# A two-layer graph attention kernel: v's last products moved up, both ends of the step loop written out anew

## The chip, the cores and the metric

The kernel runs on one core of a Trainium2 chip. The metric is device time of one execution in microseconds (us), as the median of several runs. Times inside the kernel are in us from the start of the profiled execution's span.

## The reference, cut to what matters

The input is x, 128 graphs of 128 nodes with 512 features, in float32, and an adjacency mask adj (128 x 128 for each graph). Two layers follow one another; each adds masked attention to its input and normalises the sum.

```python
# layer 0: 4 heads of 64          layer 1: 8 heads of 64, mask = adj | eye, h = layernorm(x)*gamma + beta
q, k, v = split_heads(x @ Wq), split_heads(x @ Wk), split_heads(x @ Wv)
sim  = einsum('bhid,bhjd->bhij', q, k) * 64**-0.5
attn = softmax(where(mask, sim, very_negative), axis=-1)
out  = einsum('bhij,bhjd->bhid', attn, v).reshape(...) @ Wo + bo
x    = layernorm(x + out)
```

Layer 1 computes q, k and v from a second layernorm of its input (h) with one matrix w_qkv, and its output goes through w_out. All of it is float32.

## The kernel before, in words

**Tiling.** The 128 graphs form 64 groups of two. A group's rows R[g] lie in SBUF as 128 nodes by 2 by 512. Every large product (q, k, v and the output projections) is computed by a scheme of seven products instead of eight (Strassen-Winograd): GpSimd forms sums of the left halves (`xs` and `so`, in `halves_sums`), VectorE forms differences of the weights once (`weight_sums`, `weight_sums_out`), TensorE runs products 1 to 7, and ScalarE and VectorE combine the results while they take them out of PSUM. The table `INTO` says which PSUM bank a product goes to: 1, 6, 7 and 4 accumulate one after another in bank "a", 5 and 3 in bank "f", 2 in a bank of a shared ring of four. After 1 and 6 (and 5) ScalarE copies the bank out; after 7 VectorE adds the bank to an earlier copy; after 4 ScalarE copies the bank again (`taken`, L349). So 6, 7 and 4 each wait until the engine that reads bank a after the one before has read it, and the next product 1 in that bank waits for the copy after 4. Layer 1 has `product` for q and k ("qk": banks qka, qkc, qkf in the trace) and v ("va", "vc", "vf"), layer 0 has `product_0` (all three at once: a, c, f), and the projections have `out_product` (oa, oc, of), whose seven results VectorE adds to R[g] one by one (L418).

**Stages.** The loop runs over s, 2 to 67, and each `step(s)` works on several groups at once: layer 0's q, k and v of group s, its attention (scores, masks, exponentials) of group s-1, its output and norm of group s-2, layer 1's qk of group s-2 and v of group s-3, layer 1's attention of group s-3 and its output and norm of group s-4. A step has two halves, for graph k = 2s and k = 2s+1 of the attentions.

**The attention of one graph.** `scores` fills two PSUM banks per layer. `masked` has GpSimd fill a tile sm with the very negative number (memset, L458), VectorE copy the scores over it where the mask is set (L460), and VectorE take the maximum (L463). `exps` is ScalarE's exponentials with their sums. `normalised` is a reciprocal on VectorE (L484) and a multiplication on GpSimd (L485). `blocks` turns the probabilities in 32 x 32 blocks on VectorE and writes them to DRAM (`put`), `probs_arrive` reads them back with partitions and blocks exchanged (`fetch`, tile pT), which completes the transposition. `attend` (av) multiplies pT by v; ScalarE copies the result to aT.

**The transposition of rows** goes the same way: `turn` (VectorE, L212) and a write, `arrive` the read back (tile raw), and ScalarE puts it in order: `in_order` for layer 0 (L239), `finish` for layer 1, where it also applies gamma and beta (L252), in two halves; both end with GpSimd's sums. At the ends, where the round trip has no other work beside it, `finish_direct` transposes on TensorE instead (ht).

**Order.** The schedule is written out by hand: each engine executes its instructions in the order in which the program calls them, and semaphores are set for the dependences between engines. Most work buffers (sm, xT1, raw, the sums) exist once, so a writer waits for the last reader of the group before. `finish` of the next group overwrites xT1, which v's product 4 of the group before still reads. `flush()` carries out deferred norms on ScalarE, `flush(latest)` deferred ratios on GpSimd. All DMAs are issued by SyncE, in program order.

Of the kernel before, what the change touches and what calls it, by code (L numbers as in the profile page):

```python
# [10 lines left out]
F32 = mybir.dt.float32  # L11
# [6 lines left out]
P = 128  # L18
# [9 lines left out]
def kernel(ctx: ExitStack, tc: tile.TileContext, x, adj, wq, wk, wv, wo, bo,  # L28
# [27 lines left out]
    def flush(what=later):  # L56
        while what:
            what.pop(0)()
# [95 lines left out]
    wsqk = const.tile([P, 3, KH, 2, I1 // 2], F32, name="wsqk")  # L154
    wsv = const.tile([P, 3, KH, I1 // 2], F32, name="wsv")

    def weight_sums(w, ws):
        for c in range(KH):
            if w is w1qk:
                b11, b12 = w[:, c, :, 0], w[:, c, :, 1]  # L160
                b21, b22 = w[:, KH + c, :, 0], w[:, KH + c, :, 1]
            else:
                b11, b12 = w[:, c, 0], w[:, c, 1]
                b21, b22 = w[:, KH + c, 0], w[:, KH + c, 1]
            combine(b11, b12, b21, b22, ws[:, 0, c], ws[:, 1, c], ws[:, 2, c])

    def combine(b11, b12, b21, b22, t2, t3, t4):
        nc.vector.tensor_sub(b12, b12, b11)
        nc.vector.tensor_sub(t2, b22, b12)
        nc.vector.tensor_sub(t3, t2, b11)  # L170
        nc.vector.tensor_sub(t4, b21, t2)

    def weight_sums_0():
        combine(*(w0[:, c:c + KH, h].rearrange("p c t f -> p c (t f)") for c in (0, KH) for h in range(2)),
# [253 lines left out]
    def scores(k):  # L428
        both = members(k)
        made = []  # L430
        for l, g, b in both:
            H_ = HEADS[l]

            ps = [mm_tile(f"sc{l}_{g}_{b}_{s}").rearrange("p (k n) -> p k n", n=N) for s in range(2)]
            t = slice(b * N, (b + 1) * N)
            for h in range(H_):
                r = slice((h % 2) * D, (h % 2 + 1) * D)
                if l == 0:
                    q_, k_ = (QKV[g][r, b, h // 2, i, :] for i in range(2))
                else:  # L440
                    q_, k_ = (QK[1, g][r, i * H_ // 2 + h // 2, t] for i in range(2))
                nc.tensor.matmul(ps[h % 2][:, h // 2, :], q_, k_, start=True, stop=True)  # L442
            made.append((l, g, b, ps))
        return made

    def with_self(g):

        if 0 <= g < NG:
            nc.vector.tensor_tensor(M[g], M[g], eye[:, None, :].to_broadcast([P, G, N]), op=ALU.max)

    def masked(made, layer):
        for l, g, b, ps in made:
            if l != layer:
                continue
            K = HEADS[l] // 2
            mask = M[g][:, b, :]
            sm = two.tile([P, 2, K, N], F32, tag=f"sm{l}", bufs=1, name=f"sm{l}_{g}_{b}")
            nc.gpsimd.memset(sm, (NEG0, NEG1)[l])  # L458
            for s in range(2):
                nc.vector.copy_predicated(sm[:, s], mask[:, None, :].to_broadcast([P, K, N]),  # L460
                                          ps[s][:, :K, :])
            nmax = three.tile([P, 2, K], F32, tag=f"nmax{l}", name=f"nmax{l}_{g}_{b}")
            nc.vector.tensor_reduce(nmax, sm, AX.X, ALU.max, negate=True)  # L463
            total = three.tile([P, 2, K], F32, tag=f"total{l}", name=f"total{l}_{g}_{b}")
            SM[l, g, b], SUM[l, g, b], NMAX[l, g, b] = sm, total, nmax

    def exps(l, k):
        b = k % G
# [10 lines left out]
    def normalised(k):  # L479
        for l, g, b in members(k):  # L480
            K = HEADS[l] // 2
            sm = SM[l, g, b]
            rec = three.tile([P, 2, K], F32, tag=f"rec{l}", name=f"rec{l}_{g}_{b}")
            nc.vector.reciprocal(rec, SUM.pop((l, g, b)))  # L484
            nc.gpsimd.tensor_tensor(sm, sm, rec[:, :, :, None].to_broadcast([P, 2, K, N]),  # L485
                                    op=ALU.mult)
# [38 lines left out]
    def probs_arrive(k):  # L525
        if members(k):
            fetch(*SCR.pop(("p", k)))
# [25 lines left out]
    def out_sums(l, g):  # L553
        if not 0 <= g < NG:
            return
        K = HEADS[l] // 2
        so = SO[l, g] = one.tile([P, 4, K // 2, N], F32, tag=("so", "xs0")[l], name=f"so{l}_{g}")
        halves_sums(so, AT[l, g].rearrange("p b (h c) n -> p b h c n", h=2))
# [63 lines left out]
    def p(kind, g, *which):  # L622
        for i in which:
            product(kind, g, i)

    def opening():

        transposed(0)

        for h in range(2):  # L630
            nc.scalar.activation(w0[:, :, h, 0, :], w0[:, :, h, 0, :], AF.Copy, scale=SCALE)
        product_0(0, 1)
        weight_sums_0()
        product_0(0, 2, 5, 6, 3)
        made = scores(2)
        masked(made, 0)
        exps(0, 2)
        product_0(0, 7, 4)
        normalised(2)
        blocks(2, 0, 1)  # L640
        made = scores(3)
        masked(made, 0)
        exps(0, 3)
        for _ in range(4):
            setup.pop(0)()
        load(2)
        transposed(1)
        product_0(1, 1, 5)
        normalised(3)
        blocks(3, 0, 1)  # L650
        probs_arrive(2)
        probs_arrive(3)
        for _ in range(4):
            setup.pop(0)()
        product_0(1, 2, 6, 3)
        while setup:
            setup.pop(0)()
        weight_sums_out(0)
        product_0(1, 7, 4)
        transposed(2)  # L660

    def step(s):
        k = 2 * s

        direct = s in (2, NG, NG + 1)
        load(s + 1)
        made = scores(k)
        masked(made, 0)
        masked(made, 1)
        exps(0, k)  # L670
        addend(0, s - 2)
        with_self(s - 2)
        p("qk", s - 3, 4)
        product_0(s, 1)
        attend(s)
        exps(1, k)
        out_sums(0, s - 2)
        if s >= NG:
            out_sums(1, s - 4)
        product_0(s, 5, 2)  # L680
        out_product(0, s - 2, 1, 5, 2)
        if s < NG:
            normalised(k)
            addend(1, s - 4)
            out_product(0, s - 2, 6)
            product_0(s, 6)
            blocks(k, 0)
            out_product(0, s - 2, 3, 7)
            stats(0, s - 2, 0)
            product_0(s, 3)  # L690
            out_product(0, s - 2, 4)
            stats(0, s - 2, 1)
            product_0(s, 7)
            p("v", s - 3, 1)
            blocks(k, 1)
            p("v", s - 3, 2)
            flush()
            p("v", s - 3, 5)
        else:
            p("v", s - 3, 1)  # L700
            out_product(0, s - 2, 6, 3)
            p("v", s - 3, 2)
            out_product(0, s - 2, 7)
            stats(0, s - 2, 0)
            p("v", s - 3, 5)
            out_product(0, s - 2, 4)
            stats(0, s - 2, 1)
            normalised(k)
            if s < NG + 3:
                addend(1, s - 4)  # L710
            flush()
            blocks(k, 0, 1)
        if not direct:
            turn(1, s - 2)
            arrive(1, s - 2)
        k += 1
        made = scores(k)
        masked(made, 0)
        if s == 2:
            weight_sums(w1qk, wsqk)  # L720
        p("v", s - 3, 6)
        product_0(s, 4)
        if s >= NG:
            p("v", s - 3, 3, 7, 4)
        if direct:
            finish_direct(s - 2)
        exps(0, k)
        masked(made, 1)
        exps(1, k)
        if s < NG:  # L730
            p("v", s - 3, 3)
            out_sums(1, s - 4)
        if s == NG + 2:
            addend(1, NG - 1)
        flush(latest)
        out_product(1, s - 4, 1, 5, 2)
        if s < NG:
            p("v", s - 3, 7)
        out_product(1, s - 4, 6, 3)
        if not direct:  # L740
            finish(s - 2, 0)
        if s < NG:
            p("v", s - 3, 4)
        normalised(k)
        turn(0, s + 1)
        probs_arrive(k - 1)
        if not direct:
            finish(s - 2, 1)
        out_product(1, s - 4, 7)
        stats(1, s - 4, 0)  # L750
        if s < NG + 2:
            blocks(k, 0, 1)
        else:
            blocks_direct(k)
        arrive(0, s + 1)
        if s < NG + 2:
            probs_arrive(k)
        p("qk", s - 2, 1)
        out_product(1, s - 4, 4)
        stats(1, s - 4, 1)  # L760
        p("qk", s - 2, 2, 5, 6)
        in_order(s + 1)
        if s != NG + 2:
            flush()
        p("qk", s - 2, 3, 7)
        if s == 2:
            weight_sums(w1v, wsv)
            weight_sums_out(1)

    opening()  # L770
    for s in range(2, NG + 4):
        step(s)


# [27 lines left out]
```

## Time and profile before

| What | Value |
|---|---|
| Time, median of 3 runs | 2950.45 us (2949.8 to 2950.89) |
| Span of the profiled execution | 2946.6 us, 63045 instructions, TensorE clock 0.99 |
| VectorE, ScalarE, GpSimd busy | 62%, 51%, 59% |
| DMA engines | 139 GB/s mean, 408.36 MB |
| One step in mid-run | 44.36 us (scores at 1424.52 and again at 1468.88) |
| Steps 2 and 3 (from scores to scores) | 48.43 to 86.18, 86.18 to 136.29 us |
| Steps 64 to 67 | from 2799.73 us to the end |

How to read it: a step in the middle is all work of 64 steps, so a microsecond there counts some 60 times and one at the ends once. The timeline rows shown below give the start and the duration of a merged group of instructions, the engine, the line, output tile and inputs, the count, and in brackets how long the engine was idle before them and what ended that. In rows of TensorE's waits the numbers are the total in us, how many times, and the longest. Rows of windows give busy time and instructions of TensorE, weight loads, VectorE, ScalarE and GpSimd, then the granted TensorE clock, the DMA share and GB/s.

### The profile page before, as it was taken

What the parts mean: (1) busy time and instruction counts of PE and PEld (TensorE: products, weight loads), DVE (VectorE), ACT (ScalarE), POOL (GpSimd) and SP (SyncE); (2) the same over time, 40 slices, a digit from 0 to 9 for tenths busy, and PEclk for the clock granted to TensorE, in tenths of its full rate; (3) what the DMA queues carried; (4) which work ended last, traced back from release to release, by engine and by line L of the source; (5) the groups of instructions that cost most, each with busy time, mean ns of one, the idle gap of its engine ahead of it and who ended that gap; (6) DMA issues with size and microseconds to landing.
All of it is one profiled execution on the core that took longest, in us unless ns stands there. A gap on an engine that the chain in (4) does not pass through costs nothing.

```text
span 2946.6 us, 63045 instructions
## 1 busy us (share of the span) xinstructions
PE 2846.1 (97%) x23289; PEld 2623.1 (89%) x23289; DVE 1832.0 (62%) x3623; ACT 1496.9 (51%) x4811; POOL 1752.4 (59%) x2439
## 2 busy tenths in 40 slices
PE   7899999999999999999999999999999999999986
PEld 7799999999989989999989989999999999999975
DVE  4566666666666666665666665666666666665643
ACT  3355555555555455454554555555555555455443
POOL 2466566566566566566666566566566566566643
PEclk9899999999999999999999999999999999999988
DMA  4344544544544544544545545545545545545421
GB/s 142 112 142 136 155 133 143 158 130 141 160 129 142 158 131 138 164 128 140 166 124 144 162 124 148 160 126 148 159 127 148 157 129 148 156 129 148 136 65 58
DMA packets 243427, 408.36 MB, mean 139 GB/s; under 512 B 40104, under 2 KB 176304, under 8 KB 243120
## 3 DMA queue, kind: packets, MB, share of 16 engines
q1 hardware_dynamic: 243120, 404.33, 46.1%
q8 instruction: 185, 3.03, 0.4%
q14 instruction: 122, 1.00, 0.1%
HBM read 206.57 MB, written 197.66 MB: 137 GB/s over the span
## 4 chain that ended last, share of the span: by engine, by line
PE 89%; ACT 3%; DVE 2%; POOL 2%; DMA 1%; issue 1%; SPq 1%; ACTq 0%; POOLq 0%; DVEq 0%
PE qka L321 15%; PE a L377 11%; PE oa L414 10%; PE va L321 8%; PE qkf L321 7%; PE f L377 6%; PE sc L442 6%; PE av L546 6%; PE of L414 6%; PE vf L321 4%; PE qkc L321 4%; PE c L377 3%; PE oc L414 3%; ACT xT L252 2%; PE vc L321 2%; DMA raw<-scr 1%
## 5 line engine op out<-in xcount | busy, mean ns | idle before, releaser
L476 ACT ACTIVATE sm<-sm,nmax 128x128 f32<-128x128 f32 x1536 | 595.1, 396 | 268.4 <-DVE nmax L463 268.4
L485 POOL TENSOR_TENSOR sm<-sm,rec 128x512 f32<-128x512 f32 (+1 forms) x256 | 370.7, 1468 | 486.8 <-DVE rec L484 486.8
L284 POOL TENSOR_TENSOR xs<-xT 128x256 f32<-128x256 f32 x256 | 187.0, 730 | 431.2 <-ACT xT L239 382.4
L460 DVE COPY_PREDICATED sm<-m,sc 128x512 f32<-128x512 uint8 (+1 forms) x512 | 269.6, 579 | 204.5 <-POOL sm L458 200.1
L567 POOL TENSOR_TENSOR r<-r,bias 128x1024 f32<-128x1024 f32 x128 | 303.3, 2369 | 7.2 <-ACT r L566 7.2
L476 ACT ACTIVATION_READ_ACCUMULATOR sm<-sm,nmax 128x1 f32 x1536 | 298.3, 194 | 0.0
L503 DVE STREAM_TRANSPOSE turned<-sm 128x512 f32<-128x512 f32 (+1 forms) x255 | 243.5, 970 | 50.7 <-POOL sm L485 50.1
L418 DVE TENSOR_TENSOR r<-oa,r 128x256 f32<-128x256 f32 x512 | 213.7, 417 | 71.8 <-PE oa L414 69.3
L321 PE MATMUL qkf<-xs,w 128*128 128x128 f32 x2048 | 251.3, 276 | 3.2 <-POOL xs L284 3.2
L321 PE MATMUL qka<-xs,wsqk 128*128 128x128 f32 x2048 | 249.7, 275 | 0.0
L463 DVE TENSOR_REDUCE nmax<-sm 128x4 f32<-128x512 f32 (+1 forms) x256 | 243.9, 953 | 8.8
L321 PEld LDWEIGHTS qkf<-xs,w 128*128 128x128 f32 x2048 | 240.5, 193 | 3.4 <-POOL xs L284 3.4
L321 PEld LDWEIGHTS qka<-xs,wsqk 128*128 128x128 f32 x2048 | 239.1, 192 | 0.0
L347 ACT COPY ev<-va 128x256 f32<-128x256 f32 x128 | 47.5, 371 | 354.8 <-PE va L321 354.8
L352 DVE TENSOR_TENSOR qk<-qkf,eqk 128x512 f32<-128x512 f32 x64 | 44.3, 691 | 295.0 <-PE qkf L321 295.0
L414 PE MATMUL oa<-wso,so 128*128 128x256 f32 x768 | 215.1, 389 | 11.7 <-DVE r L418 11.7
L284 POOL TENSOR_TENSOR so<-aT 128x128 f32<-128x128 f32 (+1 forms) x256 | 151.4, 592 | 116.8 <-ACT aT L551 106.1
L612 ACT ACTIVATE r<-r,shift,root 128x512 f32<-128x512 f32 x256 | 194.3, 806 | 50.4 <-POOL shift L601 50.4
L414 PE MATMUL of<-wo,so 128*128 128x256 f32 x768 | 210.3, 383 | 0.8 <-POOL so L284 0.8
L252 ACT ACTIVATE xT<-raw,gb 128x256 f32<-128x256 f32 x244 | 133.2, 594 | 108.9 <-PE va L321 108.6
L458 POOL MEMSET sm<- 128x512 f32 (+1 forms) x256 | 181.5, 738 | 0.8 <-DVE turned L503 0.8
L414 PEld LDWEIGHTS oa<-wso,so 128*128 128x128 f32 x768 | 142.5, 192 | 43.6 <-issue 26.2
(140 smaller groups left out, 6583.5 us busy)
## 6 DMA issues: line engine op xcount, KB each, us to landing
scrp<-turned SPq DMA_DIRECT2D x124, 768.0 KB, 4.3
pT<-scrp SPq DMA_DIRECT2D x496, 192.0 KB, 4.4
scr<-turned SPq DMA_DIRECT2D x122, 512.0 KB, 3.0
raw<-scr SPq DMA_DIRECT2D x488, 128.0 KB, 3.2
r<-in_x_dram SPq DMA_DIRECT2D x64, 512.0 KB, 3.7
out_dram<-r SPq DMA_DIRECT2D x64, 512.0 KB, 2.9
m<-in_adj_dram SPq DMA_DIRECT2D x64, 32.0 KB, 3.5
raw_r<-in_L_gnn_w_qkv_dram SPq DMA_DIRECT2D x8, 256.0 KB, 4.0
```

The source lines that it names most:

```text
L284: nc.gpsimd.tensor_tensor(o, a0, a1, op=op)
L321: nc.tensor.matmul(o, lhsT, rhs, start=first and n == 0, stop=n == len(todo) - 1, skip_group_check=True)
L377: nc.tensor.matmul(acc[:, t * P:(t + 1) * P], lhsT, rhs, start=first and n == 0, stop=n == len(todo) - 1, skip_group_check=True)
L414: nc.tensor.matmul(acc, left[:, c], right[:, c], start=first and c == 0, stop=c == hk - 1, skip_group_check=True)
L418: nc.vector.tensor_add(part, acc, part)
L460: nc.vector.copy_predicated(sm[:, s], mask[:, None, :].to_broadcast([P, K, N]), ps[s][:, :K, :])
L463: nc.vector.tensor_reduce(nmax, sm, AX.X, ALU.max, negate=True)
L476: nc.scalar.activation(sm[:, s, k, :], sm[:, s, k, :], AF.Exp, bias=nmax[:, s, k:k + 1], accum_out=total[:, s, k:k + 1])
L485: nc.gpsimd.tensor_tensor(sm, sm, rec[:, :, :, None].to_broadcast([P, 2, K, N]), op=ALU.mult)
L503: nc.vector.transpose(t[:, :, lo:hi, :], sm)
L567: nc.gpsimd.tensor_tensor(R[g], R[g], (bias0, bias1)[l][:, None, :].to_broadcast([P, G, E]), op=ALU.add)
L612: nc.scalar.activation(R[g][:, b], R[g][:, b], AF.Identity, bias=shift[:, b:b + 1], scale=root[:, b:b + 1])
```

## The change

It rewrites the order of the step and touches no arithmetic. In steps 4 to 63: layer 1's v products 7 and 4 move ahead of the output products 5 and 2; the copy of v's last quarter so comes ahead of all of `finish` on ScalarE; the second half's reciprocals come after two of the output adds instead of five; the turn of the next group's rows follows three more adds; the first graph's probabilities are loaded at the end of the first half instead of in the second; the memsets of both layers are issued with the scores (`cleared`); the deferred ratios come after `finish`; qk's product 2 comes ahead of output product 4, and the first statistics follow the turned blocks.

At the start: in step 2 the exponentials follow `attend`, and w's differences are split in two parts; steps 2 and 3 both use `finish_direct` (before: step 2 only), with the turn and load of the next rows ahead of it. At the end, `closing(s)` takes the place of the branches for s >= 64: reciprocals ahead of the last products of v and of the statistics, norms behind ScalarE's copy of v's product 6, memsets of both layers ahead of the addend, and in step 66 masks and exponentials ahead of the addends, the last statistics of that step deferred to step 67.

The purpose is that bank a and the masks be free before the work that needs them.

```diff
-    def weight_sums(w, ws):
-        for c in range(KH):
...
+    def weight_sums(w, ws, *parts):
+        for part in parts:
+            for c in range(KH):
...
+    def combine_1(b11, b12, b21, b22, t2, t3, t4):
         nc.vector.tensor_sub(b12, b12, b11)
         nc.vector.tensor_sub(t2, b22, b12)
+
+    def combine_2(b11, b12, b21, b22, t2, t3, t4):
         nc.vector.tensor_sub(t3, t2, b11)
         nc.vector.tensor_sub(t4, b21, t2)
...
+    def cleared(made, *layers):
+
+        for l, g, b, ps in made:
+            if l in layers:
+                sm = SM[l, g, b] = two.tile([P, 2, HEADS[l] // 2, N], F32, tag=f"sm{l}", bufs=1,
+                                            name=f"sm{l}_{g}_{b}")
+                nc.gpsimd.memset(sm, (NEG0, NEG1)[l])
...
     def masked(made, layer):
...
-            sm = two.tile([P, 2, K, N], F32, tag=f"sm{l}", bufs=1, name=f"sm{l}_{g}_{b}")
-            nc.gpsimd.memset(sm, (NEG0, NEG1)[l])
+            sm = SM[l, g, b]
...
     def step(s):
         k = 2 * s
 
-        direct = s in (2, NG, NG + 1)
+        direct = s in (2, 3)
         load(s + 1)
         made = scores(k)
+        cleared(made, 0, 1)
...
         attend(s)
+        if s == 2:
+            exps(0, k)
+        exps(1, k)
...
+        if not direct:
+            turn(1, s - 2)
+            arrive(1, s - 2)
+            probs_arrive(k)
+        k += 1
+        made = scores(k)
+        cleared(made, 0, 1)
+        masked(made, 0)
+        p("v", s - 3, 6)
+        product_0(s, 4)
+        if direct:
+            turn(0, s + 1)
+            arrive(0, s + 1)
+            probs_arrive(k - 1)
+            p("v", s - 3, 3, 7, 4)
+            finish_direct(s - 2)
+        exps(0, k)
+        masked(made, 1)
+        if s == 2:
+            weight_sums(w1qk, wsqk, combine_1)
+        exps(1, k)
+        if not direct:
+            p("v", s - 3, 3)
+        out_sums(1, s - 4)
+        out_product(1, s - 4, 1)
+        if not direct:
+            p("v", s - 3, 7)
+        out_product(1, s - 4, 5)
+        if not direct:
+            p("v", s - 3, 4)
+            finish(s - 2, 0)
+        normalised(k)
+        out_product(1, s - 4, 2, 6, 3)
+        if not direct:
+            finish(s - 2, 1)
+            turn(0, s + 1)
+        flush(latest)
+        if s == 2:
+            weight_sums(w1qk, wsqk, combine_2)
+        out_product(1, s - 4, 7)
+        blocks(k, 0, 1)
+        if not direct:
+            arrive(0, s + 1)
+        probs_arrive(k)
+        stats(1, s - 4, 0)
+        p("qk", s - 2, 1, 2)
+        out_product(1, s - 4, 4)
+        stats(1, s - 4, 1)
+        p("qk", s - 2, 5, 6)
...
+    def closing(s):
...
+        if s == NG + 3:
+            stats(1, s - 5, 1)
         out_product(0, s - 2, 1, 5, 2)
...
+        p("v", s - 3, 1)
+        out_product(0, s - 2, 6, 3)
+        normalised(k)
...
         made = scores(k)
+        p("v", s - 3, 6)
+        flush()
+        cleared(made, 0, 1)
         masked(made, 0)
...
+        if s == NG + 2:
+            masked(made, 1)
+            exps(1, k)
+        if s < NG + 3:
+            addend(1, s - 4)
         if s == NG + 2:
             addend(1, NG - 1)
+        p("v", s - 3, 3, 7, 4)
+        if s < NG + 2:
+            finish_direct(s - 2)
+            exps(0, k)
+            masked(made, 1)
+            exps(1, k)
         flush(latest)
...
+        if s != NG + 2:
+            stats(1, s - 4, 1)
...
     opening()
-    for s in range(2, NG + 4):
+    for s in range(2, NG):
         step(s)
+    for s in range(NG, NG + 4):
+        closing(s)
```

## The prediction

> **What bounds the kernel now.** I read the busy table first: TensorE 2846.1 of 2946.6 us, and 89% of the chain of waits. Then TensorE's waits, then one step's timeline, then both ends. The rows:
>
> ```profile
> PE 2846.1 (97%) x23289; PEld 2623.1 (89%) x23289; DVE 1832.0 (62%) x3623; ACT 1496.9 (51%) x4811; POOL 1752.4 (59%) x2439
> ...
> PE qka L321 <- ACT v L349: 38.0, 61, 3.5
> PE oa L414 <- DVE r L418: 12.3, 5, 6.0
> PE va L321 <- DVE v L352: 7.9, 4, 4.9
> ```
>
> One wait, 38.0 us in 61 times (one of 3.5), is the largest. In TensorE's and ScalarE's timelines of a middle step:
>
> ```profile
> 1410.28 1.03 PE L321 MATMUL va<-wsv,xT 128*128 128x256 f32 x4
> 1411.14 1.03 PE L414 MATMUL oa<-wso,so 128*128 128x256 f32 x4
> 1412.74 2.05 PE L321 MATMUL qka<-xT,w 128*128 128x128 f32 x16 [0.57 <-ACT v L349]
> ...
> 1411.34 1.09 ACT L252 ACTIVATE xT<-raw,gb 128x256 f32<-128x256 f32 x2 [1.81 <-PE va L321]
> 1412.34 0.35 ACT L349 COPY v<-va 128x256 f32<-128x256 f32 x1
> 1412.59 1.09 ACT L252 ACTIVATE xT<-raw,gb 128x256 f32<-128x256 f32 x2
> ```
>
> The last product of v (4) fills bank a; the copy that frees it stands on ScalarE behind two activations of the next group's xT, which themselves waited for that product (they overwrite the xT it reads). qka, next in bank a, starts 0.05 us after the copy. From 1000 to 1500 us TensorE is busy 493.3 of 500: 1.34%, 0.59 us of a step of 44.36 us (1424.52 to 1468.88). Nothing else stands idle in a step.
>
> The ends differ. Four pieces show it (step 3, step 64):
>
> ```profile
> 122.48 3.79 PE L321 MATMUL qka<-xT,w 128*128 128x128 f32 x16 [3.48 <-ACT v L349]
> ...
> 129.05 1.95 PE L321 MATMUL qkf<-xs,w 128*128 128x128 f32 x16
> ...
> 2822.83 2.07 PE L321 MATMUL va<-wsv,xT 128*128 128x256 f32 x4 [4.88 <-DVE v L352]
> ...
> 2835.15 1.86 PE L414 MATMUL oa<-wso,so 128*128 128x256 f32 x4 [4.95 <-DVE r L418]
> ...
> 2820.06 0.52 POOL L458 MEMSET sm<- 128x512 f32 x1
> 2831.11 0.95 POOL L458 MEMSET sm<- 128x1024 f32 x1
> ```
>
> Gaps of 3 to 6 us, and after each the same 16 matmuls last 3.79 instead of 1.95 us. The memsets stand late on GpSimd and VectorE's masks wait for them.
>
> **What the Trainium skill says.** "TensorE: Matmul & The Clock Gate", Part 1: after an idle window of about 3.4 us the array runs at half clock until it has been busy as long. The trace agrees (3.79 against 1.95), and the granted clock is 0.87 in 2800 to 2851 us against 1.00 mid-run. So I add to each long gap what the slow rows show; 0.57 us gaps cost only themselves. "PSUM — Partial Sum Buffer", Engine vs sequencer instructions: the queues of ScalarE, VectorE and GpSimd are strict FIFO; the copy behind the two activations is that. "SBUF — State Buffer", "SBUF: two separate sides": a VectorE instruction with two SBUF inputs and a GpSimd one that reads SBUF exclude each other on a shared port pair; VectorE's weight sums of wo (L168 to L171) take 1.1 to 1.2 us beside GpSimd's sums and 0.68 us alone.
>
> **Steps 4 to 63, worked out in the times of the step above.** Moves only: TensorE's order becomes oa 1, v 7, of 5, v 4, oc 2, oa 6, of 3, oa 7, qka (each 0.86 us from 1405.10).
> - v 4 goes from 1410.28 to 1407.69. It accumulates into bank a, so it needs VectorE's add of v 7 out of that bank to be over. The rows of that pair in this step, and of step 3, where 4 follows 7 directly:
>
> ```profile
> 1407.69 1.03 PE L321 MATMUL va<-wsv,xs 128*128 128x256 f32 x4
> ...
> 1408.75 0.42 DVE L352 TENSOR_TENSOR v<-va,ev 128x256 f32<-128x256 f32 x1 [0.44 <-PE va L321]
> ...
> 117.39 0.42 DVE L352 TENSOR_TENSOR v<-va,ev 128x256 f32<-128x256 f32 x1
> ...
> 117.87 1.13 PE L321 MATMUL va<-wsv,xT 128*128 128x256 f32 x4 [0.52 <-DVE v L352]
> ```
>
>   The add starts 1.06 us after the product, lasts 0.42, and the product it releases starts 0.06 after it: 1.54 us. The new order leaves two slots of 0.865, 1.73. Slack 0.2; and VectorE, busy with masks and maxima until 1405.9 and two adds until 1406.6, is free before this add is due (1407.02). No wait.
> - The v copy: exponentials end at 1409.5, copy to 1409.8. Then xT's four activations: their data, by the DMA table below, are in by about 1410. First pair to 1411.1, second to 1412.2. qka is due at 1412.0 and needs the copy and the first pair: 0.9 us early. qkc (1413.8) needs the second. **The 0.57 us goes**: (38.0 − 3.5) = 34.5 us over 60 steps.
> - Reciprocals two adds behind oa 1 instead of five: they wait for the exponentials to 1409.6, and behind them stand the adds of oc, oa 6, of 3. oa 6's is due at 1410.48 anyway and must end by 1411.14 for oa 7: it ends at 1410.9. GpSimd's multiplications move from 1411.07 to about 1409.9, the xT sums from 1413.92 to 1412.8; qkf needs them at 1416.4.
> - The turn of the next group's rows now follows three adds: ends 1413.0, not 1412.24. It heads a chain: write, read back, in_order, sums, memsets, masks, and TensorE's av needs the masked bank. Before, masks began at 1427.99 and av at 1429.38 with no wait. But the load of the first probabilities (4 of 192 KB) leaves this crowded place for an empty one:
>
> ```profile
> 1408.00:1410.00 2.00, 2.00 (x11) 1.77 (x10) 1.12 (x3) 1.53 (x8) 0.00 (x0) 1.00 0.65 169
> 1410.00:1412.00 2.00, 2.00 (x11) 1.56 (x9) 1.56 (x6) 0.66 (x2) 0.94 (x1) 1.00 0.00 0
> ...
> 1418.00:1420.00 2.00, 2.00 (x21) 2.00 (x20) 0.24 (x1) 0.58 (x1) 0.55 (x3) 1.00 0.96 375
> ```
>
> (Last columns: DMA share, GB/s.) The group's raw rows are in by 1410 and nothing moves until 1412; from 1414 to 1424 the engines are full. 768 KB at the 256 GB/s seen in 1420 to 1422 is 3 us, more than the 0.8 the turn loses. Zero. It is issued behind the raw rows' reads in the same queue, so I let these land as before.
> - The ratios on GpSimd (4 short instructions, 1.3 us) move into its idle time before in_order's sums (5.75 us idle); qk 2 before oa 4 and the statistics 2 us later end before the norms, which follow in_order. Memsets issued together: GpSimd's order in a step is as it was. All zero.
>
> **Steps 2 and 3.** Step 2 loses 2.44 us (oa waits for aT, behind exponentials that wait for a mask) and some 1.6 of slow clock; with the exponentials behind the copy, aT is early and the GpSimd addend (to 55.17) holds of to 55.7 instead of 58.03. Then 3.17 idle and 1.7 slow before qkf: xs waited for a VectorE evacuation behind eight weight sums (5.3 us). Four of these (2.7 us) now stand behind the evacuation and four (2.7) behind the reciprocals, while the turn (1.3) comes ahead of it: about 4 us earlier, and qkf then waits some 0.6 for w's first differences. 0.85 us is still idle before of. So 2.9 and 4.2: 7. Step 3 starts with 3.98 us behind the v and wo sums, still there: 1. Its later 3.48, plus 3.0 slow, come from the round trip over DRAM; group 1 now is transposed on TensorE (8 transposes, 1.0 us as in step 2), evacuated by about 120.2, so qka starts some 2.3 us sooner and at full clock: 5. **Head 13.**
>
> **Steps 64 to 67.** Here VectorE's order sets the pace, so I replayed step 64 with the durations of its own rows. Reciprocals stand after five adds: 2810, when the exponentials end, not 2813.2. GpSimd's multiplications (2.9 us) end at 2813.0 instead of 2817.8, its four short roots at 2815.0; VectorE's transposes of the probabilities (0.7 and 1.2 us, behind the statistics) at 2815.1; both memsets (0.5 and 0.95) follow by 2816.4, not 2820.58 and 2832.06, the addend behind them instead of before. Mask 0.8, maximum 0.7, adds of v 3 and v 7 0.7: v 4 starts at 2817.8, not 2822.83. Of these 5.0 and the 1.46 idle before v 7, that idle goes because ScalarE's copy of v 6 now stands ahead of the norms (1.5 us). Then ht, its evacuation to 2821.4, masks and maximum of layer 1 (2.5) with no wait for a memset, and the add that oa 6 waits for: 2824.3, not 2835.15. The three rows after it lose their slow clock (4.36 us instead of 2.6): 12 in all. Step 65 alike: oa 6 from 2881.85 to 2874, 10 with slow rows. Step 66: masks and exponentials move before the v adds: v 4 waits about 3 us longer, the addends come after the exponentials, pt moves from 2924.79 to about 2925.5: −1. Step 67: the deferred statistics let GpSimd's last sums start without 1.6 us of roots: +1. Sum 22; gaps of 2 us remain, and some may still slow the clock: I take **18**.
>
> Sum: 34.5 + 13 + 18 = 65.5, so 2950.45 − 65.5 = **2885**.
>
> **Rivals.**
> - A: a new wait in each step. v 4's slack is 0.2 us, oa 7's 0.24; a miss of the same size would lose 0.3 to 0.6 us in 60 steps: 18 to 36 back, near 2912. For: thin slacks. Against: the latencies are read from this kernel and repeat in every step.
> - B: the ends pay nothing, each gap replaced by the next (long chains over four engines): 34.5 and some 4, about 2912.
> - C, slower: the moved probability load shares the engines with the raw rows, which land up to 3 us later; the first xT pair ends at 1414, qka waits 2.0 instead of 0.57: 60 × 1.4 = 86 lost, 31 won at the ends: about 3005. Against: issued behind, and the engines empty after 1410.
>
> **Chances.** Forecast 0.70 (2872 to 2899), A 0.12, B 0.10, C 0.08, where a smaller delay could also cancel (within 0.2%: 0.02) or lose (0.06). Faster 0.92. The low end is every gap paid in full: 35.6 + 16 + 26 = 78, 2872; the high end takes in most of A and B: 2913.
>
> **What would show it.** Right: qka's wait on v gone from TensorE's waits, step period near 43.8 us, TensorE near 100% mid-run; in step 64 memsets about 4 us after the reciprocals; no 3 us gap in step 3. Wrong: a wait of va on v or oa on r repeated 60 times (A); waits of xT on raw and qka on xT (C); gaps of the old size past 2760 us (B).

## The result, and the profile after

| What | Before | After |
|---|---|---|
| Time, median of 4 runs each on one chip | 2950.12 us (2947.17 to 2950.89) | 2865.48 us (2865.0 to 2865.81) |
| Ratio | | 0.9715, 95% interval 0.9698 to 0.9732 |
| Span of the profiled execution | 2946.6 us | 2863.7 us |
| Step in mid-run, scores to scores | 44.36 us | 43.51 us (2696.86 to 2740.37) |
| Scores of step 2, 3, 4, 64 start at | 48.43, 86.18, 136.29, 2799.73 | 48.98, 79.56, 125.61, 2740.37 |

The kernel is 84.6 us faster, below the low end of the range (2872). Of the 82.9 us between the two spans, 10.7 lie ahead of step 4 (136.29 − 125.61), 48.7 in steps 4 to 63 and 23.5 from step 64 on (146.9 us before, 123.3 after).

The busy row of the changed kernel's page, and a window of 500 us in mid-run, whose first pair of numbers is TensorE's busy time and instructions:

```profile
PE 2818.6 (98%) x23297; PEld 2614.6 (91%) x23297; DVE 1824.1 (64%) x3625; ACT 1502.7 (52%) x4811; POOL 1758.7 (61%) x2439
```

```profile
1000.00:1500.00 500.00, 500.00 (x4190) 465.16 (x4192) 323.54 (x645) 270.00 (x865) 318.48 (x439) 1.00 0.49 144
```

TensorE is at 500.00 of 500 us, where it was at 493.3 before, and a step is 1.9% shorter (43.51 against 44.36 us). Its busy share in the page hardly moves, because the array was already called busy for 97% of the time. What is left of its waits (total us, times, longest):

```profile
PE va L328 <- DVE v L359: 7.2, 4, 4.7
PE oa L421 <- DVE r L425: 5.5, 5, 1.7
...
PE av L560 <- DVE sm L474: 4.4, 1, 4.4
...
PE qka L328 <- ACT eqk L354: 2.0, 1, 2.0
PE pt L534 <- POOL sm L499: 1.8, 1, 1.8
PE av L560 <- DMA pT<-scrp: 1.8, 1, 1.8
```

The row of qka on v (38.0 us in 61 times) is gone, nothing repeats 60 times, and each wait shown belongs to steps 2 and 3, to the last four, or to the start of step 4. The place in a middle step, TensorE and ScalarE:

```profile
2724.38 1.03 PE L328 MATMUL va<-wsv,xT 128*128 128x256 f32 x4
...
2727.83 1.03 PE L421 MATMUL oa<-wso,so 128*128 128x256 f32 x4
2728.70 1.95 PE L328 MATMUL qka<-xT,w 128*128 128x128 f32 x16
2730.48 1.95 PE L328 MATMUL qkc<-xT,w 128*128 128x128 f32 x16
...
2726.13 0.36 ACT L356 COPY v<-va 128x256 f32<-128x256 f32 x1
2726.38 2.09 ACT L259 ACTIVATE xT<-raw,gb 128x256 f32<-128x256 f32 x4
```

The copy of v (product 4) stands ahead of all four activations of xT, bank a is free 2.2 us before qka is due, and qka starts 0.87 us after the product ahead of it. The first pair of xT, which qka reads too, is the closer of the two: it is done 1.2 us ahead.

The ends, TensorE's rows that waited longest (steps 3, 4, 64 and 66):

```profile
88.91 1.98 PE L560 MATMUL av<-pT,qkv 128*64 128x128 f32 x16 [4.42 <-DVE sm L474]
...
120.08 2.02 PE L328 MATMUL qka<-xs,wsqk 128*128 128x128 f32 x16 [1.98 <-ACT eqk L354]
...
132.93 1.08 PE L560 MATMUL av<-pT,qkv 128*64 128x128 f32 x8 [1.80 <-DMA pT<-scrp]
...
2758.32 1.13 PE L328 MATMUL va<-wsv,xT 128*128 128x256 f32 x4 [1.45 <-DVE v L359]
...
2764.61 1.13 PE L421 MATMUL oa<-wso,so 128*128 128x256 f32 x4 [1.70 <-DVE r L425]
...
2832.36 1.52 PE L328 MATMUL va<-wsv,xT 128*128 128x256 f32 x4 [4.67 <-DVE v L359]
```

In step 64 two waits of nearly 5 us have become 1.45 and 1.70, and the four matmuls after them run in 1.13 us, not in 1.86 to 2.07. The granted clock over steps 64 and 65 is 1.00 where it was 0.88. The first wait of step 3 has not shrunk, and steps 3, 4 and 66 have waits that were not there, or were smaller.

### The profile page after: what moved, and what is told of

Its sections match the earlier page's. It is cut to its first block, busy times and chain, and to the rows that moved or that the text cites. A ratio compares the mean times of both kernels' runs of the same rounds, so it can differ in the third digit from the quotient of the medians.

```text
span 2863.7 us, 62995 instructions
## 1 busy us (share of the span) xinstructions
PE 2818.6 (98%) x23297; PEld 2614.6 (91%) x23297; DVE 1824.1 (64%) x3625; ACT 1502.7 (52%) x4811; POOL 1758.7 (61%) x2439
## 4 chain that ended last, share of the span: by engine, by line
PE 96%; DVE 2%; POOL 1%; ACT 1%; DMA 0%; issue 0%; SPq 0%; ACTq 0%; POOLq 0%; DVEq 0%
PE qka L328 16%; PE oa L421 12%; PE a L384 12%; PE va L328 8%; PE qkf L328 8%; PE sc L449 7%; PE f L384 6%; PE av L560 6%; PE of L421 6%; PE qkc L328 4%; PE vf L328 4%; PE c L384 3%; PE oc L421 3%; PE vc L328 2%; ACT sm L490 0%
## 5 line engine op out<-in xcount | busy, mean ns | idle before, releaser
L581 POOL TENSOR_TENSOR r<-r,bias 128x1024 f32<-128x1024 f32 x128 | 303.0, 2367 | 10.7 <-ACT r L580 10.7
L354 ACT COPY eqk<-qka 128x512 f32<-128x512 f32 x128 | 75.1, 587 | 205.4 <-PE qka L328 205.4
L219 DVE STREAM_TRANSPOSE turned<-r 128x512 f32<-128x512 f32 x242 | 163.8, 697 | 26.3 <-ACT r L626 26.2
```

Source lines behind the costliest of these rows:

```text
L581: nc.gpsimd.tensor_tensor(R[g], R[g], (bias0, bias1)[l][:, None, :].to_broadcast([P, G, E]), op=ALU.add)
```

## The experiments

The question was why each of the 60 middle steps gave 0.85 us when the shown wait was 0.57, and which parts of the change are needed for it. Each kernel ran on the same chip as the kernel before, but not all on one chip. The kernel before took 2948.0 to 2950.1 us there, so that small differences between two rows of the table, up to some 2 us, say little. By the label of a wait I mean the idle time in brackets at its row; v 7 or out 3 is product 7 of layer 1's v or product 3 of the output projection (oa, oc, of).

| Kernel | Time, us | Ratio to before, 95% interval |
|---|---|---|
| before, v's products alone moved | 2969.71 | 1.0068 (1.0051 to 1.0085) |
| before, v's products and the load moved | 2898.11 | 0.9828 (0.9813 to 0.9843) |
| after, v's products back | 2933.11 | 0.9946 (0.9931 to 0.9961) |
| after, load back | 2932.06 | 0.9942 (0.9927 to 0.9957) |
| after, v's copy late | 2962.94 | 1.0049 (1.0034 to 1.0064) |
| after, reciprocals back | 2870.66 | 0.9734 (0.9718 to 0.9750) |
| after, memsets back | 2882.24 | 0.9776 (0.9762 to 0.9791) |
| after, old start | 2874.61 | 0.9748 (0.9733 to 0.9763) |
| after, old end | 2887.76 | 0.9794 (0.9779 to 0.9808) |
| after, waits in the ends removed | 2854.60 | 0.9679 (0.9663 to 0.9695) |

### The products of v back

```diff
-        out_product(1, s - 4, 1)
-        if not direct:
-            p("v", s - 3, 7)
-        out_product(1, s - 4, 5)
-        if not direct:
-            p("v", s - 3, 4)
-            finish(s - 2, 0)
+        out_product(1, s - 4, 1, 5)
         normalised(k)
-        out_product(1, s - 4, 2, 6, 3)
+        out_product(1, s - 4, 2)
         if not direct:
+            p("v", s - 3, 7)
+        out_product(1, s - 4, 6, 3)
+        if not direct:
+            finish(s - 2, 0)
+            p("v", s - 3, 4)
             finish(s - 2, 1)
```

> The changed kernel with one edit undone: in steps 4 to 63 v's products 7 and 4 stand again behind output products 2 and 3, and the copy of v between the two halves of finish. The rest as changed. Theory 1: period 44.36 again, 51 us more than the changed kernel, about 2916. Theory 2: 34 more, about 2900, period 44.08, since the edit that brings the other 0.28 stays in. Theory 3: as theory 1 or less.

Measured: 67.6 us more than the changed kernel, 1.13 a step, more than any of the three theories has. Its waits, then its timeline:

```profile
PE qka L328 <- ACT v L356: 34.5, 60, 0.6
```

```profile
1408.71 1.03 PE L421 MATMUL of<-wo,so 128*128 128x256 f32 x4
1409.76 1.13 PE L328 MATMUL va<-wsv,xT 128*128 128x256 f32 x4
1410.72 1.03 PE L421 MATMUL oa<-wso,so 128*128 128x256 f32 x4
1412.33 2.05 PE L328 MATMUL qka<-xT,w 128*128 128x128 f32 x16 [0.58 <-ACT v L356]
```

Go by starts, not by labels. These products start 0.865 us apart when nothing holds them, but a row lasts 1.03, so 0.17 us of a wait behind such a row lies under it and is not in the label. oa to qka is 1.61 us, 0.74 more than 0.865, of which 0.58 is labelled. The 16 matmuls after the wait take 2.05 instead of 1.95, 0.1 more (why they do, no run shows). Together that is the 0.85. And v 4 here starts 1.05 us after its forerunner, 0.19 late, with no label at all; that and its own slower start (1.13 instead of 1.03) make the rest of the 1.13. VectorE shows why v 4 is late:

```profile
1408.86 0.20 DVE L498 RECIPROCAL rec<-total 128x8 f32<-128x8 f32 x1 [2.03 <-ACT sm L490]
...
1409.29 0.42 DVE L359 TENSOR_TENSOR v<-va,ev 128x256 f32<-128x256 f32 x1
```

The reciprocals, which wait for the exponentials, stand ahead of the add of v 7 here, and v 4 starts 0.05 us after that add. So this kernel is not quite the old order: in the kernel before the add came first, and a step cost 0.85, not 1.13.

### A known delay

```diff
-            p("v", s - 3, 4)
+            product("v", s - 3, 4, take=False)
             finish(s - 2, 0)
...
             finish(s - 2, 1)
+            for c in range(2):
+                nc.scalar.activation(junk, RAW[1][:, :, :, c, :], ...)
+            taken("v", s - 3, 4, ACC["v", "a"])
```

> The changed kernel with one known wait put in: ScalarE copies v's product 4 out only after all of finish and two more activations of finish's size into a scratch tile (which nothing reads), in steps 4 to 63. The copy then ends near 2729.6 where it ended at 2726.5 in the trace, and qk's product 1, which started at 2728.70, follows it: 0.96 us later from start to start, of which the records should show about 0.8 as idle. Theory, idle labels understate: a step costs 0.96 plus 0.1 for the slow first matmuls, 1.05 to 1.1 us, 2928 to 2932. Rival, the label is the cost (0.8 a step): 2911 to 2915. Prediction's rival A in another form, that nothing may be late there: same direction, no number.

Measured: 97.5 us more, 1.62 a step, beyond both. The timeline holds the answer:

```profile
1200.09 1.03 PE L422 MATMUL oa<-wso,so 128*128 128x256 f32 x4
1201.88 2.05 PE L328 MATMUL qka<-xT,w 128*128 128x128 f32 x16 [0.77 <-ACT v L357]
```

```profile
1783.47 1.03 PE L422 MATMUL oa<-wso,so 128*128 128x256 f32 x4
1786.73 3.03 PE L328 MATMUL qka<-xT,w 128*128 128x128 f32 x16 [2.23 <-ACT v L357]
```

In steps like the first (label 0.77, the commonest) the scores are 44.55 us apart, 1.04 more than in the changed kernel: the label plus 0.27, as the theory says. The sum missed because about half of the steps wait longer, up to 2.5 us: there `finish` itself starts late, behind raw rows that land later in some steps (ScalarE waits 1.36 us for them ahead of the second row), and a copy behind all of `finish` passes that on. Beyond 0.77 us each, the labels add to 26 us, and after five of the long waits the matmuls also run slowly, as in the second row (see the end). So ScalarE's new order gives a second thing: the copy no longer depends on a DMA.

### The products alone, and the load

The kernel before with products 7 and 4 of v moved, and nothing else:

```diff
-        out_product(1, s - 4, 1, 5, 2)
+        out_product(1, s - 4, 1)
         if s < NG:
             p("v", s - 3, 7)
-        out_product(1, s - 4, 6, 3)
-        if not direct:
-            finish(s - 2, 0)
+        out_product(1, s - 4, 5)
         if s < NG:
             p("v", s - 3, 4)
+        out_product(1, s - 4, 2, 6, 3)
+        if not direct:
+            finish(s - 2, 0)
```

> The kernel before with one edit: v's products 7 and 4 moved up behind output products 1 and 5, and so the copy of v ahead of all of finish on ScalarE. Everything else, both ends too, as before. Theory 1 (the wait of a step costs what the starts of the matmuls show, 0.85 us: 0.74 from product oa to qka beyond its 0.86, and 0.11 in the first matmuls of qka): step period 43.51 us, 60 x 0.85 = 51 less, about 2899 us. Theory 2 (the wait costs the 0.57 us that its row shows, and another edit of the step brings the other 0.28): period 43.79, about 2916. Theory 3 (the copy is early enough only together with the other moves, such as the earlier load of the probabilities): a new wait of qka or av in the step, above 2916.

Measured: 2969.71, slower than before, as in theory 3. The wait of qka is gone and another has come, in 60 places. Its waits, then TensorE, ScalarE and VectorE in one step:

```profile
PE av L546 <- DVE sm L460: 76.2, 60, 4.0
```

```profile
1430.61 0.71 PE L442 MATMUL sc<-qkv 64*128 64x128 f32 x8
...
1436.48 1.09 PE L546 MATMUL av<-pT,qkv 128*64 128x128 f32 x16 [0.94 <-DVE sm L460]
...
1431.23 1.14 ACT L239 COPY xT<-raw 128x512 f32<-128x512 f32 x2 [3.45 <-DMA raw<-scr]
...
1435.98 0.78 DVE L460 COPY_PREDICATED sm<-m,sc 128x256 f32<-128x256 uint8 x2 [4.58 <-POOL sm L458]
```

Read backwards: av waits for a mask, the mask for GpSimd's memset, which stands behind the sums of xT, which wait for the raw rows. The turn that starts this chain ended 10.6 us ahead of these scores, where it was 12.3 before. TensorE, without its wait, comes to these scores 0.85 us sooner. The rest, 0.87, is the turn's: it stands behind the add of out 3, and out 3 is now one product later, since v 4 goes ahead of it. (No more adds stand ahead of the turn than in the kernel before, here or in the changed kernel. The section on the change has that wrong; what delays the turn is this product.) The rows land 11 us after the turn in both. In the changed kernel they take 8.4 (turn ends 1380.8, `in_order` at 1389.18). SyncE issued, in this kernel and then in the changed one:

```profile
1420.06 0.34 SPq L197 DMA_DIRECT2D scr<-turned  x1
1420.51 2.21 SPq L203 DMA_DIRECT2D pT<-scrp  x4
...
1423.57 3.21 SPq L203 DMA_DIRECT2D raw<-scr  x4
```

```profile
1380.81 0.34 SPq L204 DMA_DIRECT2D scr<-turned  x1
...
1383.58 2.54 SPq L210 DMA_DIRECT2D raw<-scr  x4
```

Is it the load of the probabilities (pT), which stands between the turn's write and the read of the raw rows in the first of these?

```diff
             arrive(1, s - 2)
+            if s < NG:
+                probs_arrive(k)
         k += 1
...
         turn(0, s + 1)
-        probs_arrive(k - 1)
+        if direct or s >= NG:
+            probs_arrive(k - 1)
```

> The kernel before with two of the change's parts only: v's products 7 and 4 moved up, and the first graph's probability load issued at the end of the first half (steps 3 to 63). Reciprocals, memsets, the turn's place and both ends stay as before. Theory, load pays for the products: with the products alone the turn ends 10.6 us ahead of the next scores (12.3 in the kernel before) and the raw rows reach ScalarE 11.1 us after it; in the changed kernel they take 8.4, because the probability load is no longer in the queue between. So the load's move gives back 2.6 to 2.7 us, attend's wait on the masks goes, the step falls to 43.5 us, and the time is that of the changed kernel plus what its two ends gave (22.3 and 9.1): 2895 to 2901. Rival, the reciprocals or the turn behind finish are needed too: the wait stays in part, a step of 44.0 to 44.3, 2920 to 2945. My prediction, which gave the load nothing: 2969, as with the products alone.

Measured: 2898.11, within the theory's 2895 to 2901. With these two parts the middle steps are those of the changed kernel: 43.51 us as a rule, and 3.1 us more in all of steps 5 to 63. The reverse, the load alone back in the changed kernel:

```diff
             arrive(1, s - 2)
-            probs_arrive(k)
...
             turn(0, s + 1)
+            probs_arrive(k - 1)
```

> The changed kernel with the first graph's probability load back in its later place, behind the turn, in steps 4 to 63. Theory, load pays: the raw rows come 2.6 us later; attend's first product has 1.9 us to spare on the first mask (mask ends 1394.4, product starts 1396.3), so it waits some 0.7 us a step, with what the records hide 0.7 to 1.0: 2907 to 2925, and a wait of attend on the masks appears in most steps. Prediction (the move is worth zero): 2865 to 2868.

Measured: 2932.06, 66.6 more, on the theory's side but past its 2925. Its TensorE waits, and ScalarE's:

```profile
PE av L560 <- DVE sm L474: 65.9, 59, 4.4
```

```profile
ACT xT L246 <- DMA raw<-scr: 210.0, 59, 4.9
```

And ScalarE's in the changed kernel:

```profile
ACT xT L246 <- DMA raw<-scr: 49.0, 59, 2.2
```

ScalarE's wait for the raw rows is 3.56 us in the mean; it is 0.83 in the changed kernel. The 2.7 us was right; that one step's 1.9 us to spare held for all was not (1.06 is left to wait in the mean). Of the 65.9 us, 4.4 belong to step 3. In steps 5 to 63 the labels add to 61.5 us in 58 waits, and these steps are 66.2 us longer than 43.51 each: here a label hides 0.08 us, not the 0.28 of qka's, since the row ahead of av reaches only 0.07 us under it and av itself runs no slower.

### Reciprocals, memsets

```diff
-        normalised(k)
         out_product(1, s - 4, 2, 6, 3)
+        normalised(k)
```

> The changed kernel with the reciprocals of steps 2 to 63 back behind the five adds of the second half (behind the adds of out 2, 6 and 3). Theory and prediction (their move is worth nothing in these steps; the kernel with products and load alone already ran at the changed kernel's step): 2863 to 2868. Rival, the reciprocals pay, since GpSimd's multiplications, its sums of xT for qk's product 5 and the turned probabilities come 1.5 us later: a wait of 0.2 to 0.5 us a step, 2877 to 2895.

Measured: 2870.66, some 5 us more, a little above the theory's range and well below the rival's; the interval overlaps that of the changed kernel. The step is 43.51 us as a rule. In the trace attend waits for masks 8 times, 10.7 us, not once for 4.4, since everything behind the adds, the turn too, comes a little later; steps 5 to 63 take 7.2 us more in all. The reciprocals' place gives slack that a few steps use, not time in each step.

```diff
     def masked(made, layer):
...
+            cleared([(l, g, b, ps)], l)
...
-        cleared(made, 0, 1)
```

> The changed kernel with each memset of a masked bank again issued right ahead of its own masks, as in the kernel before, in all steps. Theory and prediction for steps 4 to 63: GpSimd's order in a step is the same or nearly so, nothing moves. At the ends the memset of layer 1 in steps 64 and 65 again stands behind GpSimd's addend, which only now precedes it: out 6's wait (1.7 us each) grows by 0 to 3 us. Together 2865 to 2872. Rival, the memsets' place is a main part of what the ends gave (22.3 us): 2876 to 2886.

Measured: 2882.24, the rival's number. No middle step changed (43.51). From step 64 on it is 12.7 us longer; 2.9 more are lost by step 5: step 3 is 7.2 us longer, and step 4 gives 3.7 of that back. TensorE and GpSimd, step 3 and step 64:

```profile
123.79 3.75 PE L328 MATMUL qka<-xs,wsqk 128*128 128x128 f32 x16 [6.13 <-ACT eqk L354]
...
2771.86 2.04 PE L421 MATMUL oa<-wso,so 128*128 128x256 f32 x4 [5.96 <-DVE r L425]
...
2767.81 0.95 POOL L464 MEMSET sm<- 128x1024 f32 x1
```

In the changed kernel both memsets of that half stand here (its step 64 starts at 2740.37):

```profile
2755.55 1.42 POOL L464 MEMSET sm<- 128x512 f32 x2
```

With the memsets back, layer 1's stands behind the addend and the direct turn's sums again: it ends 25.4 us after the step's scores (2743.36), in the changed kernel 16.6 after. The masks wait for it, and the adds that out 6 needs stand behind the masks.

### The ends put back one at a time

Steps 64 to 67 as in the kernel before (`step_old` for s >= 64):

> The changed kernel with steps 64 to 67 in the order of the kernel before. If the three stretches add up as the two traces show them (23.5 us from the scores of step 64 to the end): about 2889. By the prediction's 18: 2883.5. If the old end depends on what the old steps leave behind, neither.

Measured: 2887.76, 22.3 more than the changed kernel and near the 2889 of the traces. Steps 2 and 3 as before (`step_old` for s < 4):

> The changed kernel with steps 2 and 3 in the order of the kernel before. If the stretches add up as the two traces show them: step 4's scores come 10.7 us later, and step 4 no longer waits for the probabilities (1.8 us and slow matmuls behind, about 3 us in the changed kernel): between 2873 and 2876. By the prediction's 13: 2878.5.

Measured: 2874.61, 9.1 more (its runs lie between 2872.4 and 2876.8). What the start gives is step 2: 30.6 us in all eight traces with the new order, 37.8 to 37.9 in the four with the old. Step 3 has to be taken with step 4, whose attend waits for the probabilities that step 3 writes (1.80 us in the changed kernel, no wait in this one). Steps 3 and 4 together take 93.25 us in the changed kernel, 91.72 in the one with the old end, which runs the same instructions there, and 48.14 + 43.52 = 91.66 in this one. So no gain from the new order of step 3 is shown.

Ends and middle add up, within the spread of the runs: 2865.5 + 22.3 + 9.1 = 2896.9, and the kernel with the old ends and only the two parts of the middle took 2898.1.

### A version that beats both

```diff
+        if s == 3:
+            weight_sums(w1v, wsv, combine_1, combine_2)
...
+        if s == 3:
+            exps(0, k)
...
+        if s == 3:
+            weight_sums_out(1)
...
-            weight_sums(w1v, wsv, combine_1, combine_2)
-            weight_sums_out(1)
...
+        if s == NG + 2:
+            addend(1, s - 4)
         exps(0, k)
...
-        p("v", s - 3, 3, 7, 4)
+        p("v", s - 3, 3, 7)
+        if s == NG + 2:
+            masked(made, 1)
+        p("v", s - 3, 4)
...
         normalised(k)
+        if s == NG + 2:
+            addend(1, NG - 1)
```

> The changed kernel with the waits left in its ends taken away: v's weight sums stand in step 3 behind attend and the output weights' sums behind step 3's last masks, not ahead of step 3's first masks; step 3's first-layer exponentials of the second graph ahead of the direct turn; in step 66 v's products 3 and 7 ahead of the masks, layer 1's addend of graph pair 62 at the step's start and that of 63 behind the reciprocals. Theory, the waits are the cost: step 3 loses its 4.4 us wait of attend and the 2.0 us wait of qk's product 6; step 66 loses 4.7 (v 4), 1.4 (out 6) and part of 1.8 (turn of the probabilities), together 12 to 14: 2851 to 2854. Rival, each wait is followed by the next one (probabilities' load in step 4, the exponentials in step 66), half of it comes back: 2857 to 2861.

Measured: 2854.60, 10.9 below the changed kernel, between the ranges of the theory (2851 to 2854) and the rival. Waits and TensorE's rows:

```profile
PE va L328 <- DVE v L359: 3.5, 4, 1.4
PE pt L534 <- POOL sm L499: 2.3, 1, 2.3
```

```profile
114.72 2.02 PE L328 MATMUL qka<-xs,wsqk 128*128 128x128 f32 x16 [1.97 <-ACT eqk L354]
...
2830.25 1.97 PE L534 MATMUL pt<-ident,sm 128*128 128x128 f32 x8 [2.27 <-POOL sm L499]
```

Attend's wait of 4.4 us is gone and step 3 takes 41.0 us instead of 46.05, step 4 45.5 instead of 47.2. In step 66 v 4 waits 1.0 us instead of 4.7, and from its scores to attend it is 25.1 us instead of 29.9. What I had from the earlier exponentials of step 3 (2.0) did not come: ScalarE still copies eqk behind the layer 1 exponentials. And the turn on TensorE in step 66 (pt) waits 0.5 us longer, and its eight matmuls take 1.97 us after that wait, in the changed kernel 1.09.

## Why the prediction was right and wrong

The direction and the mechanism of steps 4 to 63 were right: the wait of qka went, and no other came to TensorE in its place. The sizes, by its own terms:

- **"The 0.57 us goes: (38.0 − 3.5) = 34.5 us over 60 steps"** is the step that failed. It measured 48.7. The prediction took the idle label as the wait, and said that "0.57 us gaps cost only themselves". The label starts at a modelled end of the matmuls ahead, and the busy share that seemed to confirm it (0.59 us of a step) is made of the same ends. In the trace of before the starts were there to read, with this row behind the three that the prediction shows:

```profile
1414.63 1.03 PE L414 MATMUL oa<-wso,aT 128*128 128x256 f32 x4
```

  1411.14 to 1412.74 is 1.60 for 0.865, and 1412.74 to 1414.63 is 1.89 for 16 matmuls that otherwise start the next work after 1.78. 0.74 and 0.11 are 0.85. Steps 5 to 63 gave 51.5 us, 0.85 each and 1.4 from some longer steps of the kernel before; step 4, with its new wait, lost 2.8. The Trainium skill, "Perfetto Trace Analysis", Tensor Engine Instruction, says that TensorE's profiled end is an estimate, "so the TE profile time is a model, not a measurement". This case agrees, and gives the amount: labels of 0.57 and 0.77 stood for 0.85 and 1.04, both 0.27 to 0.28 more.
- **Steps 64 to 67, "Sum 22 … I take 18"**: 23.5 in the trace, 22.3 in the run with the old end. Step 64 to its qka gave 12.9 for the 12 of the replay, step 65 10.5 for 10, step 66 lost 0.4 for 1, step 67 gave 0.6 for 1. The replay from the rows' own durations held: it put v 4 and out 6 of step 64 at 18.1 and 24.6 us after the step's scores, and they came at 17.95 and 24.24. The discount for a clock that might stay slow had no row behind it. The memsets, part of that replay, carry 12.7 us of it.
- **"Head 13"**: 10.7. Step 2 gave 7.2 for 7. Step 3 gave 4.1 for 6, and of that the prediction can claim little. The step-3 qka after the round trip has no wait now, as said. But the wait of 3.98 did not shrink by 1; it is 4.42, since one of VectorE's sums of w1v (0.41 us alone) took 2.58 beside GpSimd's addend. And a wait of 1.98 came that the prediction didn't see: the exponentials now follow `finish_direct` on ScalarE, and the copy that frees bank a follows them. In this trace that wait was not followed by slow matmuls; in four others with the same step 3 it was, and the step took 48.5 to 49.1 us there instead of 46.05. What step 3 gains, step 4 then waits for, and the prediction has no term for that. Step 2 also began 0.55 us later.
- **The load and the turn, "Zero"**: right as a sum, wrong as a reason. The pair of products and load is needed: either alone costs more than a us a step (76.2 us of attend's waits with the products alone). The working had the turn lose 0.8 us; against the next scores it lost 1.6 to 1.7, because the step that it saves is also a step that the round trip over DRAM has less time for.
- **Reciprocals**: small in time, though not nothing: some 5 us in the whole run. **Rival C** was closer than the result looks, for another reason than its own. `finish` does wait for layer 1's raw rows in 17 steps, 9.8 us in all (before once, 0.3). But it does so as often with the load back in its old place (17 times, 8.7 us), so the moved load is not the cause; in the kernel before it was v 4 that held `finish` back (108.6 us in 60 times), and the new order took that away. qka needs the first pair of xT, which has 1.2 us to spare, and the longest of these waits used all of it:

```profile
1770.33 2.08 ACT L259 ACTIVATE xT<-raw,gb 128x256 f32<-128x256 f32 x4 [1.13 <-DMA raw<-scr]
...
1771.42 1.95 PE L328 MATMUL qka<-xT,w 128*128 128x128 f32 x16
```

  The pair ended as qka was due. In the kernels with the products alone and with products and load, one such wait in mid-run did hold qka up (0.47 and 0.60 us). That none did here is in part luck.

The three errors of size add to +14.2 + 5.5 − 2.3 = 17.4 us, the 82.9 of the spans less the 65.5 of the sum.

## What to carry to other kernels

Price a TensorE wait from the starts of the groups on both sides, against the same pair where nothing waits, and not from the idle label. What the label leaves out depends on the rows around it, not on its length: here 0.28 us at each wait of qka, half of the label again, and 0.08 at each of attend's. When a change shortens a loop, check the longest chain that runs round it through other engines and DRAM, since it gets the same shorter time. Leave a replay from measured durations as it comes out; a discount needs a row of its own. And compare a step together with the one that waits for what it writes: step 3 alone looked 4 us better.

## What was not expected of the hardware

- An idle time of about 2 us can slow the clock, and need not. In the kernel with the late copy 12 waits of qka lasted 1.87 us or longer. After five of these (1.87, 1.88, 1.93, 2.23 and 2.46 us) the 16 matmuls took 2.47 to 3.43 us and the granted clock was 0.76 over 7 us; after the other seven, 1.89 to 2.37 long, they took 2.05 and the clock was 1.00. Two of them:

```profile
1155.00:1162.00 7.00, 6.29 (x38) 6.19 (x39) 2.56 (x4) 1.24 (x3) 3.48 (x8) 0.76 0.89 282
795.00:802.00 7.00, 6.68 (x56) 6.58 (x57) 3.55 (x7) 1.01 (x4) 3.55 (x9) 1.00 0.87 274
```

  Even one wait in one place goes both ways. Step 3's wait for eqk is 1.97 or 1.98 us in seven kernels; the 16 matmuls after it took 2.02 us in three of them, the changed kernel among these, and 2.97 to 3.60 in four, such as the one with the load back:

```profile
120.28 3.13 PE L328 MATMUL qka<-xs,wsqk 128*128 128x128 f32 x16 [1.97 <-ACT eqk L354]
```

  "TensorE: Matmul & The Clock Gate", Part 1 of the Trainium skill, gives an idle window of about 3.4 us; here gaps of 1.8 to 2.5 us sometimes sufficed (1.80 ahead of attend in step 4 of the changed kernel), so the length alone doesn't decide. What else does, no run shows. (The prediction's 3.79 us "after each" gap is that of one row; the groups of four matmuls that it shows took 2.07 and 1.86.)
- Loads ahead of a read delay it by more than the later issue. In the kernel with the products alone the raw rows were issued 3.51 us after the turn's write, in the changed kernel 2.77, but they came 11.2 and 8.4 us after the turn. The load of 768 KB between them is the cause, since moving it alone has the same effect (2.7 us in the mean of 59 steps); whether it holds the rows up by its place in the queue or by sharing the DMA engines, no run separates.
